# Three more output tiles turned on VectorE from quartered loads, instead of on TensorE: a planner's two thresholds

## The chip, the cores and the metric

The kernel runs on one core of one Trainium2 chip. The metric is the device time of one execution in microseconds (us), given as the median of several runs; lower is better. One further execution was taken with the hardware profiler on, and every row of a profile shown here is of that one.

The engines are named as the profile names them: PE is TensorE (matrix products), PEld its weight loads, DVE is VectorE, ACT is ScalarE, POOL is GpSimd, SP is SyncE. A name with a q at its end (SPq, ACTq) is the engine's queue of instructions that issue transfers (DMAs).

## The reference

One attention layer over a graph of 2708 nodes with 1024 features, all in float32:

```python
def reference(x, adj, W_q, b_q, W_k, b_k, W_v, b_v):
    h = jnp.maximum(_layernorm(x, axis=-1), 0.0)
    q = h @ W_q.T + b_q
    k = h @ W_k.T + b_k
    v = h @ W_v.T + b_v
    z = (1.0 / math.sqrt(1024)) * (q @ k.T)
    z = z * adj                                   # adj: 0 or 1, about 4 ones in a row
    z = jnp.where(z == 0.0, -10000.0, z)
    return x + relu(softmax(z, axis=1) @ v)
```

## The kernel before

**The shape of the work.** A row of `adj` holds about four ones, so no full 2708x2708 product is made. The kernel first finds the ones of each row, sorts the rows by their count, and cuts the sorted rows into 21 tiles of 128 rows (and a short last one). W_q and W_k are multiplied into one matrix M beforehand. From then on each tile t goes through three stages: its query `q = h M` (a product on TensorE), its attention, and its output `relu(u W_v)` plus x (a product on TensorE again).

**Attention of a tile** is VectorE's work. GpSimd gathers the neighbours' rows of h, one neighbour for each of the 128 rows at a time (line 610, a tile `g` of 128x1024, or a free piece of `M`). VectorE forms one score for each gathered tile (line 863), ScalarE the exponentials (line 872), VectorE the weights (lines 906 to 911), ScalarE the first term of the weighted sum (line 912), and VectorE the other terms (line 923). The result is `u`, 128 rows of 1024. A gathered tile lies in one of eleven slots (later thirteen); a slot comes free for the next gather when its term of the sum has been added.

**Products run in units of two tiles.** Twenty units stand in a list: units 0 to 9 make q of two tiles each, units 10 to 19 the output of two tiles each, in the order of the list `order`; the last tile, 8, is done alone behind them. The sixth output pair is unit 15 (tiles 18 and 12), the seventh is unit 16 (tiles 19 and 11). A unit is one level of Strassen's scheme: seven block products of four matmuls of 128x512 (`add_block`, line 1011) instead of eight. Its operands `a11`, `a12`, `a22` and `s1` to `s4` are 128x512 blocks of the two tiles transposed, and their sums (`blocks`). They are made one unit ahead: for unit n+1 the function `upper` runs at step 0 of unit n and `lower` at step 2. The first product that uses them is at step 5 of unit n.

**Two ways to transpose.** `is_faced` decides for each tile:

- By TensorE: eight transposes of 128x128 against the identity (`half_turned`, line 415) into PSUM, and ScalarE copies out (`held`, line 718) for `a11`, `a12` and `a22`; VectorE reads the fourth half from PSUM in its sums (line 722).
- By VectorE ("faced"): VectorE transposes only within 32x32 blocks, so the blocks have to be moved to their places by the transfers. ScalarE permutes the columns of `u` into `v` (line 945), its queue stores `v` to `u_dram` (line 947), SP's queue loads it back by quarters in four transfers of 32x4x256 (`by_quarters`, line 700), and VectorE makes two transposes of 128x512 (`faces`, line 705).

A tile turned by TensorE is handed over in one of two ways. If its unit is at most two units ahead when it is finished (`near`), `u` stays on chip. Otherwise SP's queue stores it (line 951) and loads it back in whole rows (line 1212).

**What sets the order.** VectorE's order is written out by the program: attention is a generator (`attention`), and at each of the seven steps of a unit `advance(share)` takes from it as many steps as the budget `share` allows. The budget is 20.9/7 or 21.5/7 us for a step, less 2.3/7 us for each faced tile of the next unit, whose transposes VectorE has to make in the same stretch:

```python
share = (20.9 if n < len(units) - 5 else 21.5) / 7
if nxt is not None and nxt[0] == "o":
    share -= 2.3 / 7 * len(set(nxt[1:]) & faced_tiles)
```

The other engines' orders are made by a scheduler when the program is built. `load_rows` brings unit n+2's tiles at step 4 of unit n. Whether a tile is faced is settled in `sums`, when the program order reaches its last term: `now` is the unit and step reached there, `unit` the tile's own unit, `len(q_pairs)` is 10.

**The end.** Tile 8 is faced: VectorE's last term for it is at line 929, then ScalarE's copy, the store, four loads, and one transpose into `T_alone` (line 705). TensorE uses `T_alone` first at the `between` of unit 19. Late in unit 19 TensorE also runs a small product `ps_f` (line 1353) from `many`, a count that VectorE makes at lines 1339 to 1351; its result decides whether a general fallback must run.

Of the kernel before, what the change touches and what calls it, by code (L numbers as in the profile page):

```python
# [65 lines left out]
def tile_preln_masked_attention(  # L66
# [144 lines left out]
    def row_tile(name):  # L211
        return work.tile([P, D], FT, tag="row", name=name, bufs=ROWS)
# [626 lines left out]
    def fill():  # L839
        while wanted and free:  # L840
            t, s = wanted.pop(0)
            g = free.pop(0)
            if s == K[t]:
                half = slice(HOSTS.index(t) * HP, (HOSTS.index(t) + 1) * HP)
                nc.gpsimd.dma_start(g[:HP], v_dram[half, :])
            else:
                with tc.issue_after(first_q[0].ins) if first_q else nullcontext():
                    gathered.append(gather(g, h_dram[:, :], t, s, P, skip=True))
            g_of[t].append(g)

    def chained(step):

        with tc.issue_after(chain[-1].ins):
            chain.append(step())
# [64 lines left out]
    def sums(t):  # L919
        u, coef, m = us.pop(t)  # L920
        for s in range(0 if t in EMPTY else 1, K[t]):
            fill()
            chained(lambda: nc.vector.scalar_tensor_tensor(  # L923
                u, g_of[t][s], coef[:, s:s + 1], u, op0=ALU.mult, op1=ALU.add))
            free.append(g_of[t][s])
            yield 1.3
        fill()
        if t in HOSTS:
            chained(lambda: nc.vector.scalar_tensor_tensor(
                u[:HP], g_of[t][K[t]][:HP], m[:HP, 3:4], u[:HP], op0=ALU.mult, op1=ALU.add))  # L930
            free.append(g_of[t][K[t]])
            yield 1.3
            fill()
        g_of.pop(t)
        if t == SECOND:
            nc.sync.dma_start(v_dram, u)
            whole_second.append(True)
            return
        unit = next((n for n, pair in enumerate(units) if pair[0] == "o" and t in pair[1:]), len(units))
        if now < [unit - 2, 2] and unit <= len(q_pairs) + 4 or unit >= len(units) - 1:  # L940
            faced_tiles.add(t)
        print("done", t, "at", now, "unit", unit, t in faced_tiles)
        if t in faced_tiles:
            v = row_tile(f"v_{t}")
            nc.scalar.copy(v.rearrange("p (a c r) -> p c a r", a=QUADS, r=QP),
                           u.rearrange("p (c a r) -> p c a r", a=QUADS, r=QP))
            nc.scalar.dma_start(u_dram[t * P:(t + 1) * P, :], v)
        elif near(t):
            held[t] = u
        else:  # L950
            nc.sync.dma_start(u_dram[t * P:(t + 1) * P, :], u)
        done.add(t)
# [7 lines left out]
    def attention(order):  # L960
        for t in order[:2]:
            ask(t)
        free.extend(slots)

        fetch(order[0])
        fill()
        yield 0.0
        marked(0, EARLY)
        yield 0.0
        after = order[1:] + [None, None]  # L970
        yield from scores(order[0], after[0])
        for i, t in enumerate(order):
            nxt = after[i]
            ahead = nxt is not None and K[t] + K[nxt] <= HIGH + 1
            part = scores(nxt, after[i + 1]) if nxt is not None else iter(())
            if ahead:

                for _ in range(min(2, K[nxt] - 1)):
                    yield next(part, 0.0)
            weights(t)  # L980
            yield 0.6
            if ahead:
                yield from part
            yield from sums(t)
            yield from part
# [8 lines left out]
    spent, now = [0.0], [0, 0]  # L994

    def near(t):

        return t == alone or any(t in unit[1:] for unit in units[:now[0] + 3] if unit[0] == "o")
# [193 lines left out]
    q_pairs = [(t, t + 1) for t in range(0, BARE, 2)]  # L1192
    o_pairs = [(order[i], order[i + 1]) for i in range(0, FULL - 1, 2)]
    alone = order[-1]
    units = [("q",) + p for p in q_pairs] + [("o",) + p for p in o_pairs]
# [367 lines left out]
```

## Time and profile before

| | us |
|---|---|
| median of 3 runs | 638.43 (636.95 to 638.96) |
| the profiled execution, its own time | 638.0 |
| the profiled execution, span from the first to the last instruction | 636.3 |
| TensorE busy | 624.6 (98% of the span) |
| VectorE busy | 525.7 (83%) |
| GpSimd busy | 361.8 (57%) |
| ScalarE busy | 283.5 (45%) |

The granted clock of TensorE is 0.995 over the span. In the timeline an instruction's row begins with its start and its duration in us; "x8" is the number of neighbours merged into the row, and brackets at the end tell how long the engine was idle before it and what ended that. A matmul of 128x512 in float32 shows as two records. A row's duration reaches to the end of its last instruction, so rows of one engine overlap a little: what an instruction holds its engine for is read from one row's start to the next.

### The profile page before, as it was taken

Reading aid. Unit: us, or ns where it says so; the run is one execution under the profiler, and the core shown is the slowest. Engines: PE = TensorE matmul, PEld = TensorE weight load, DVE = VectorE, ACT = ScalarE, POOL = GpSimd, SP = SyncE. Lnnn points to the kernel's source line nnn. Section 1 sums busy time; section 2 is a strip of 40 time slices with the busy share of each in tenths; the row PEclk is TensorE's granted clock in tenths of the full one; section 3 lists DMA queues with packets and bytes.
Section 4 is the critical chain, followed back from the end, with each engine's and each line's share of the span. In section 5 each row is a group of like instructions: output and inputs, shape, how many; then the busy total and the mean of one; then the engine's idle time right before and its main releaser. Section 6 shows DMA issues by size and latency. Waiting matters only on the chain.

```text
span 636.3 us, 6139 instructions
## 1 busy us (share of the span) xinstructions
PE 624.6 (98%) x1627; PEld 315.5 (50%) x1627; DVE 525.7 (83%) x1021; ACT 283.5 (45%) x421; POOL 361.8 (57%) x383
## 2 busy tenths in 40 slices
PE   9999999999999999999999999999999999999994
PEld 5777766444444544444444434444444444444441
DVE  5999889897995755997889999999999989898341
ACT  3539975859667533424341243443343333422300
POOL 2649960975868277563742563576566777632431
PEclk9999999999999999999999999999999999999997
DMA  8998897598696439986699998999999999893761
GB/s 339 407 372 310 334 351 298 199 342 328 246 382 221 170 113 334 326 299 196 194 289 323 297 412 216 311 318 324 351 378 321 334 299 295 242 289 95 210 217 40
DMA packets 62352, 180.11 MB, mean 283 GB/s; under 512 B 10039, under 2 KB 17031, under 8 KB 61672
## 3 DMA queue, kind: packets, MB, share of 16 engines
q0 software_dynamic: 25136, 78.41, 39.4%
q1 hardware_dynamic: 31242, 80.19, 35.8%
q10 hardware_dynamic: 5934, 21.06, 8.5%
q8 instruction: 15, 0.25, 0.2%
q14 instruction: 25, 0.20, 0.1%
HBM read 147.23 MB, written 42.31 MB: 298 GB/s over the span
## 4 chain that ended last, share of the span: by engine, by line
PE 85%; DVE 6%; issue 4%; DMA 3%; SPq 1%; POOL 0%; ACT 0%; POOLq 0%; DVEq 0%; ACTq 0%
PE ps L1011 38%; PE psy L1011 28%; PE ps_y L476 6%; PE ps_x L476 4%; PE ps_z L476 4%; PE pt L415 3%; DVE u L923 2%; DMA g<-h_dram,tab 1%; DMA or<-u_dram 1%; DVE junk L863 1%; DVE s L722 1%; DVE wlow L1270 1%; PE ps_y L511 1%; SPq L700 1%; DVE q L1092 0%
## 5 line engine op out<-in xcount | busy, mean ns | idle before, releaser
L610 POOL DMA_INDIRECT g<-h_dram,tab x94 | 121.4, 1291 | 84.4 <-DVE u L923 31.1
L1011 PE MATMUL ps<-M,a 128*128 128x512 f32 x320 | 144.0, 593 | 0.0
L1011 PE MATMUL psy<-wlow,s 128*128 128x512 f32 x320 | 143.9, 592 | 0.0
L863 DVE SCALAR_TENSOR_TENSOR junk<-g,pq 128x1024 uint8<-128x1024 f32 x93 | 113.7, 1222 | 14.0 <-DMA g<-h_dram,tab 10.9
L1011 PEld LDWEIGHTS ps<-M,a 128*128 128x128 f32 x320 | 59.8, 190 | 70.8 <-issue 70.6
L1011 PEld LDWEIGHTS psy<-wlow,s 128*128 128x128 f32 x320 | 59.7, 190 | 70.2 <-issue 69.4
L923 DVE SCALAR_TENSOR_TENSOR u<-g,coef,u 128x1024 f32<-128x1024 f32 x69 | 88.4, 1281 | 6.9 <-ACT u L912 5.8
L389 DVE FIND_INDEX8 at<-ones,adj 128x8 uint32<-128x685 f32 (+1 forms) x88 | 74.5, 865 | 0.0
L1011 PE MATMUL psy<-wlow,a 128*128 128x512 f32 x160 | 72.0, 593 | 1.4 <-DVE q L1092 1.4
L1011 PE MATMUL ps<-M,s 128*128 128x512 f32 x160 | 72.1, 592 | 0.0
L1011 PE MATMUL ps<-wlow,s 128*128 128x512 f32 x160 | 72.0, 593 | 0.1
L368 ACT ACTIVATE sized<-adj 128x2708 uint8<-128x2708 f32 (+1 forms) x22 | 54.3, 2468 | 7.5 <-DMA adj<-in_adj_dram 6.2
L298 POOL TENSOR_TENSOR hsum<-hsum,x 128x256 f32<-128x256 f32 (+1 forms) x56 | 38.7, 729 | 25.6 <-DVE wlow L444 21.2
L1110 POOL DMA_INDIRECT y<-in_x_dram,tab x19 | 34.8, 1832 | 29.1 <-ACT y L1127 15.9
L1011 PEld LDWEIGHTS psy<-wlow,a 128*128 128x128 f32 x160 | 30.3, 190 | 40.0 <-issue 37.1
L1011 PEld LDWEIGHTS ps<-wlow,s 128*128 128x128 f32 x160 | 30.3, 190 | 38.6 <-issue 37.9
L1011 PEld LDWEIGHTS ps<-M,s 128*128 128x128 f32 x160 | 30.3, 190 | 38.1 <-issue 37.4
L912 ACT ACTIVATE u<-g,coef 128x1024 f32<-128x1024 f32 x18 | 20.7, 1147 | 32.1 <-DVE coef L911 32.1
L808 POOL DMA_INDIRECT out_dram<-y,tab x21 | 25.0, 1188 | 16.4 <-DVE flag L1354 6.1
L626 POOL DMA_INDIRECT tab_dram<-tab,pos_i x22 | 21.9, 995 | 20.7 <-DVE pos_i L689 15.3
L276 ACT ACTIVATE x<-x,r 128x1024 f32<-128x1024 f32 (+1 forms) x22 | 25.9, 1235 | 7.3 <-POOL r L266 7.3
L760 ACT COPY ps<-bp_sb 128x512 f32<-128x512 f32 x42 | 24.5, 595 | 7.2 <-DVE y L1145 6.7
(251 smaller groups left out, 843.5 us busy)
## 6 DMA issues: line engine op xcount, KB each, us to landing
adj<-in_adj_dram SPq DMA_DIRECT2D x21, 1354.0 KB, 11.3
x<-in_x_dram SPq DMA_DIRECT2D x21, 512.0 KB, 3.9
h_dram<-x ACTq DMA_DIRECT2D x21, 512.0 KB, 8.7
u_dram<-v ACTq DMA_DIRECT2D x13, 512.0 KB, 6.4
or<-u_dram SPq DMA_DIRECT2D x52, 128.0 KB, 7.0
q_late<-q SPq DMA_DIRECT2D x12, 512.0 KB, 6.0
pq<-q_late SPq DMA_DIRECT2D x12, 512.0 KB, 8.6
M<-in_wv_dram SPq DMA_DIRECT2D x4, 1024.0 KB
```

The lines of the kernel that those rows point to most:

```text
L276: nc.scalar.activation(xs[i][:n], xs[i][:n], AF.Relu, bias=r[:n, 4, i:i + 1], scale=r[:n, 3, i:i + 1])
L298: small.append(nc.gpsimd.tensor_add(hsum[:n, cols], hsum[:n, cols], xt[:n, cols]))
L368: nc.scalar.activation(sized[:n], a[:n, :, :PW], AF.Abs, accum_out=total[:n, t:t + 1])
L389: nc.vector.max_index(at[:n, k - first_k, g, :], ones[:n, 0:8], a[:n, g, :])
L476: mm = nc.tensor.matmul(bank, a_tile(o + H * a[0], a[1], i), b(o), start=first and o == 0, stop=(o == H - 1), skip_group_check=True)
L610: return nc.gpsimd.indirect_dma_start(out=dst, out_offset=None, in_=src, in_offset=off, bounds_check=N - 1, oob_is_err=False)
L760: nc.scalar.copy(return_[h], row[:, h * NB:(h + 1) * NB])
L808: to = nc.gpsimd.indirect_dma_start(out=out, out_offset=bass.IndirectOffsetOnAxis(ap=ptab.bitcast(U32)[:n, t, SLOTS:SLOTS + 1], axis=0), i ...
L863: chained(lambda: nc.vector.scalar_tensor_tensor(junk, g_of[t][s], 1.0, tq[t], op0=ALU.mult, op1=ALU.mult, accum_out=zall[:, t, s:s + 1]))
L923: chained(lambda: nc.vector.scalar_tensor_tensor(u, g_of[t][s], coef[:, s:s + 1], u, op0=ALU.mult, op1=ALU.add))
L1011: mm = nc.tensor.matmul(bank, a[:, c, :], b[:, c, :], start=False, stop=(c == 3), skip_group_check=True)
L1110: return nc.gpsimd.indirect_dma_start(out=y[:n], out_offset=None, in_=x, in_offset=off, compute_op=ALU.add)
```

## The change

Two numbers in the rule of `sums` are changed:

```diff
         unit = next((n for n, pair in enumerate(units) if pair[0] == "o" and t in pair[1:]), len(units))
-        if now < [unit - 2, 2] and unit <= len(q_pairs) + 4 or unit >= len(units) - 1:
+        if now < [unit - 2, 1] and unit <= len(q_pairs) + 6 or unit >= len(units) - 1:
             faced_tiles.add(t)
```

Before, units 10 to 14 could be faced; now 10 to 16. With the step changed from 2 to 1 the rule takes tiles 18 and 12 (unit 15; finished at unit 12, steps 2 and 6) and tile 19 (unit 16; finished at unit 13, step 3). Tile 11, finished at unit 14, step 1, is not taken and stays with TensorE. Units 10 to 14 and 17 to 19 keep their way of turning.

Since unit 14 now has two faced tiles ahead and unit 15 one, the budget of attention is smaller in those two units, and attention steps move to later places of VectorE's order. Tile 15 is now finished at unit 15, step 0, instead of unit 14, step 5; by then its unit 17 is near, so it is handed over on chip and is not stored and loaded any more.

On TensorE, around units 14 and 15. The rows are matmuls by their outputs and inputs; `or` is a tile loaded back, `u` a tile handed over on chip, `pt` the PSUM tile that takes the transposes. Before:

```order
L1011 MATMUL psy<-wlow,a_2740 128x512 x4
L415 MATMUL pt<-ident,or_2928 128x128 x8
L1011 MATMUL psy<-wlow,s_2879 128x512 x4
L415 MATMUL pt<-ident,or_2930 128x128 x8
L1011 MATMUL ps_2908<-M,a_2856 128x512 x4
L1011 MATMUL ps_2910<-M,s_2881 128x512 x4
L1011 MATMUL psy<-wlow,s_2874 128x512 x4
L1011 MATMUL ps_3058<-M,a_2996 128x512 x4
L1011 MATMUL ps_3060<-wlow,s_3039 128x512 x4
L1011 MATMUL psy<-wlow,a_2872 128x512 x4
L415 MATMUL pt<-ident,or_3089 128x128 x8
L1011 MATMUL psy<-wlow,s_3043 128x512 x4
```

The same place of the changed kernel:

```order
L1011 MATMUL psy<-wlow,a_2742 128x512 x4
L1011 MATMUL psy<-wlow,s_2883 128x512 x4
L1011 MATMUL ps_2914<-M,a_2860 128x512 x4
L1011 MATMUL ps_2916<-M,s_2885 128x512 x4
L1011 MATMUL psy<-wlow,s_2878 128x512 x4
L1011 MATMUL ps_3047<-M,a_3003 128x512 x4
L1011 MATMUL ps_3049<-wlow,s_3024 128x512 x4
L1011 MATMUL psy<-wlow,a_2876 128x512 x4
L1011 MATMUL psy<-wlow,s_3027 128x512 x4
L415 MATMUL pt<-ident,u_2929 128x128 x8
```

Three groups of eight transposes are gone (tiles 18, 12 and 19); tile 11's, the last row, stays. Nothing else moves on TensorE.

On VectorE, in unit 14, where the operands of unit 15 are made. `u` is a running sum of attention, `junk` a score, `a` and `s` operands. Before:

```order
L923 TENSOR_SCALAR u_2923<-M,coef,u_2923 128x1024 x2
L863 TENSOR_SCALAR junk_3008,zall<-g_1413,pq_2963 128x1024
L863 TENSOR_SCALAR junk_3010,zall<-g_1403,pq_2963 128x1024
L906 TENSOR_SCALAR w_2977,m_3018<-w_2977,keys 128x4
L910 RECIPROCAL m_3018<-m_3018 128x1
L911 TENSOR_SCALAR coef<-w_2977,m_3018 128x4
L863 TENSOR_SCALAR junk_3025,zall<-g_1404,pq_2963 128x1024
L722 TENSOR_TENSOR s_3039<-a_3032,pt 128x512
L722 TENSOR_TENSOR s_3041<-a_2996,pt 128x512
L722 TENSOR_TENSOR s_3043<-s_3039,a_2996 128x512
L722 TENSOR_TENSOR s_3045<-a_3003,s_3043 128x512
```

Now:

```order
L923 TENSOR_SCALAR u_2929<-M,coef,u_2929 128x1024
L705 STREAM_TRANSPOSE a_3003<-or_2934 128x4x4x32
L705 STREAM_TRANSPOSE a_3005<-or_2934 128x4x4x32
L923 TENSOR_SCALAR u_2929<-M,coef,u_2929 128x1024
L863 TENSOR_SCALAR junk_3010,zall<-g_1413,pq_2975 128x1024
L863 TENSOR_SCALAR junk_3018,zall<-g_1403,pq_2975 128x1024
L705 STREAM_TRANSPOSE a_3020<-or_2939 128x4x4x32
L705 STREAM_TRANSPOSE s_3022<-or_2939 128x4x4x32
L722 TENSOR_TENSOR s_3024<-a_3020,s_3022 128x512
L742 TENSOR_TENSOR s_3022<-a_3003,s_3022 128x512
L722 TENSOR_TENSOR s_3027<-s_3024,a_3003 128x512
L722 TENSOR_TENSOR s_3029<-a_3005,s_3027 128x512
```

Four transposes have come in; the four sums are as many as before but read no PSUM tile, and the weights and a score (lines 906 to 911, 863) have moved behind them. In unit 15 two transposes come in likewise.

On VectorE at the end, in unit 19: `T_alone`, the results of unit 19 (`y`, `u`, `p`) and the count (`zs`, `many`). Before:

```order
L705 STREAM_TRANSPOSE T_alone<-or_3698 128x4x8x32
L1145 TENSOR_SCALAR y_3703<-ps_3655,y_3703 128x512
L1339 TENSOR_SCALAR zs<-zall,keys 128x352
L1340 TENSOR_TENSOR zs<-zall 128x352
L1341 TENSOR_SCALAR zs<-zs 128x352
L1342 TENSOR_REDUCE many<-zs 128x1
L1155 TENSOR_TENSOR u_3716<-ps_3657,u_3716 128x512
L1349 TENSOR_TENSOR many<-many,deg 128x1
L1145 TENSOR_SCALAR y_3703<-u_3716,y_3703 128x512
L1351 TENSOR_TENSOR many<-many,deg 128x1
L1151 TENSOR_TENSOR p_3691<-psy,p_3691 128x512
L1145 TENSOR_SCALAR y_3704<-p_3691,y_3704 128x512
```

Now:

```order
L705 STREAM_TRANSPOSE T_alone<-or_3681 128x4x8x32
L1145 TENSOR_SCALAR y_3686<-ps_3638,y_3686 128x512
L1155 TENSOR_TENSOR u_3699<-ps_3640,u_3699 128x512
L1339 TENSOR_SCALAR zs<-zall,keys 128x352
L1145 TENSOR_SCALAR y_3686<-u_3699,y_3686 128x512
L1151 TENSOR_TENSOR p_3674<-psy,p_3674 128x512
L1340 TENSOR_TENSOR zs<-zall 128x352
L1145 TENSOR_SCALAR y_3687<-p_3674,y_3687 128x512
L1341 TENSOR_SCALAR zs<-zs 128x352
L1342 TENSOR_REDUCE many<-zs 128x1
L1349 TENSOR_TENSOR many<-many,deg 128x1
L1351 TENSOR_TENSOR many<-many,deg 128x1
```

The last step of `many` (line 1351) now stands behind the sum into `y_3687`, the second tile of unit 19, and with it behind the gather of x for that tile; before it stood ahead of it.

## The prediction

> **What bounds the kernel now.** I read the page's busy times and chain first, then TensorE's waits and its timeline, then busy times by unit, then VectorE's waits, and last the end of the program. From the page:
>
> ```profile
> span 636.3 us, 6139 instructions
> ...
> PE 624.6 (98%) x1627; PEld 315.5 (50%) x1627; DVE 525.7 (83%) x1021; ACT 283.5 (45%) x421; POOL 361.8 (57%) x383
> ...
> PE 85%; DVE 6%; issue 4%; DMA 3%; SPq 1%; POOL 0%; ACT 0%; POOLq 0%; DVEq 0%; ACTq 0%
> ```
>
> TensorE is the bound: 98% busy, and 85% of the chain that ended last. After 360 us it waits once (its waits from 360 us to the end: us in total, times, longest):
>
> ```profile
> PE psy L1011 <- DVE q L1092: 1.4, 1, 1.4
> ```
>
> That wait is for a q, so it lies before unit 10, where the program's order is the same in both kernels, and it stays. Unit 14's first steps in TensorE's timeline, with the transposes of tiles 18 and 12 in between:
>
> ```profile
> 468.78 1.04 PE L415 MATMUL pt<-ident,or 128*128 128x128 f32 x8
> 469.65 3.60 PE L1011 MATMUL psy<-wlow,s 128*128 128x512 f32 x8
> 473.09 1.04 PE L415 MATMUL pt<-ident,or 128*128 128x128 f32 x8
> 473.96 3.60 PE L1011 MATMUL ps<-M,a 128*128 128x512 f32 x8
> ```
>
> Whatever TensorE no longer does here shortens the program, if TensorE still waits for nothing. VectorE is the engine to watch. Busy times of unit 13, of unit 14, of units 14 to 17 together and of unit 18 (after the stretch and its length come PE, PEld, DVE, ACT, POOL, then PE's granted clock, the DMA engines' share, GB/s):
>
> ```profile
> 444.70:468.80 24.10, 24.10 (x58) 10.61 (x57) 23.01 (x41) 7.99 (x14) 14.01 (x10) 1.00 1.04 370
> 468.80:494.60 25.80, 25.80 (x74) 12.31 (x73) 23.55 (x40) 9.73 (x17) 18.05 (x15) 1.00 1.01 328
> 468.80:571.90 103.10, 103.10 (x289) 49.21 (x288) 93.86 (x145) 38.26 (x65) 67.90 (x53) 1.00 0.96 302
> 571.90:595.90 24.00, 24.00 (x57) 10.64 (x56) 19.76 (x36) 8.26 (x13) 5.96 (x4) 1.00 0.45 114
> ```
>
> Units 14 to 17 turn two tiles each on TensorE and take 103.1/4 = 25.8 us each; units 13 and 18 turn none and take 24.0 to 24.1. TensorE is busy in all of it. VectorE is busy 93.9 of the 103.1 us (91%): it has little room. The DMA engines' share is 0.96 to 1.04 up to unit 17, so transfers are tight too.
>
> **TensorE: what goes.** Three groups of eight transposes. A group holds TensorE from 468.78 to 469.65, and from 473.09 to 473.96: 0.87 us each. Three groups are **2.6 us**. The units agree: 25.8 less 24.0 to 24.1 is 1.7 to 1.8 for two groups. By the records' own mean the answer is another:
>
> ```profile
> L415 PE MATMUL pt<-ident,or 128*128 128x128 f32 x32 | 4.1, 272 | 0.0
> ```
>
> 24 x 272 ns would be 6.5 us. But the records overlap: eight of them pass in 0.87 us, 109 ns each. I take the starts, since they add up to the unit's length, and keep 6.5 for a rival. [...]
>
> **VectorE: what comes.** Two transposes of 128x512 for each tile. Tiles 17 and 13, unit 14's, take this way already and show the price:
>
> ```profile
> 447.23 1.30 DVE L705 STREAM_TRANSPOSE a<-or 128x512 f32<-128x512 f32 x2
> 448.45 1.18 DVE L863 SCALAR_TENSOR_TENSOR junk<-g,pq 128x1024 uint8<-128x1024 f32 x1
> ...
> 452.68 0.71 DVE L705 STREAM_TRANSPOSE a<-or 128x512 f32<-128x512 f32 x1 [0.49 <-DMA or<-u_dram]
> ```
>
> From 447.23 to 448.45 is 1.22 us for a tile, 3.66 us for three (1.22/8 = 153 ns for each 128x128). The sums of `lower` are as many as before. So VectorE has 3.66 us more, in front of everything it still does for attention. Will tile 8, the last, be late by that? Only as far as VectorE's waits don't shrink. The waits of VectorE between 470 and 592 us, grouped (us in total, times, longest):
>
> ```profile
> DVE u L923 <- ACT u L912: 2.8, 2, 1.6
> DVE junk L863 <- DMA M<-h_dram,tab: 1.8, 1, 1.8
> DVE junk L863 <- DMA g<-h_dram,tab: 1.8, 2, 1.0
> DVE p L1122 <- ACT taken L1076: 1.2, 2, 1.0
> DVE s L722 <- ACT a L718: 1.0, 1, 1.0
> ```
>
> The last two groups hang on TensorE's pace, through ScalarE's copies of its results: 1.2 + 1.0 = 2.2 us. A VectorE that is later, beside a TensorE that is earlier, no longer has them. The two for gathers are 1.8 + 1.8 = 3.6 us. A later VectorE finds them landed, but it also frees the slots later; I take half, 1.8. The first group is two round trips to ScalarE and stays. So 2.2 + 1.8 = 4.0 us can be given back, a little more than the 3.66 that come, and tile 8 ends about when it ends now. Call its lateness d: bounds -2.1 (all of 5.8 given back) and +3.7 (nothing given back); I take 0, near the -0.3 that these rows give.
>
> **The end: what d costs.** Here TensorE comes 2.6 us earlier to something that VectorE and a chain of transfers deliver:
>
> ```profile
> 591.14 1.27 DVE L929 SCALAR_TENSOR_TENSOR u<-g,m,u 64x1024 f32<-64x1024 f32 x1
> ...
> 605.03 1.25 DVE L705 STREAM_TRANSPOSE T_alone<-or 128x1024 f32<-128x1024 f32 x1 [11.56 <-DMA or<-u_dram]
> ...
> 607.75 0.53 DVE L1341 SCALAR_TENSOR_TENSOR zs<-zs 128x352 f32<-128x352 f32 x1
> ...
> 609.26 0.19 PEld L1011 LDWEIGHTS ps<-M,T_alone 128*128 128x128 f32 x1 [0.24 <-issue]
> ...
> 610.07 0.15 DVE L1351 TENSOR_TENSOR many<-many,deg 128x1 f32<-128x1 f32 x1
> 610.14 0.68 DVE L1151 TENSOR_TENSOR p<-psy,p 128x512 f32<-128x512 f32 x1
> 610.86 0.69 DVE L1145 SCALAR_TENSOR_TENSOR y<-p,y 128x512 f32<-128x512 f32 x1
> ...
> 616.55 0.28 PE L1353 MATMUL ps_f<-many,ones 128*128 128x1 f32 x2
> ```
>
> `T_alone` is ready at 605.03 + 1.25 = 606.3; TensorE loads it at 609.3, a margin of 3.0. With TensorE 2.6 earlier (606.7) the margin is **0.4 us**. TensorE then stalls for d - 0.4 us, and the gain is 2.6 less that. At d = 0 it is whole.
>
> **Small terms, each costed at nothing.** `many` moves behind `y<-p`, which needs x's gather. That row ran at 610.86 without a wait, so the gather had landed; behind it come 0.7 for the sum itself, about 0.5 each for lines 1341 and 1342 and 0.15 each for lines 1349 and 1351, 2.0 in all, so `many` ends at about 612.9, and TensorE comes to `ps_f` at 616.55 - 2.6 = 613.9. Cover 1.0 us; with a late d it is gone too, but the stall at `T_alone` has then pushed TensorE back by as much. ScalarE loses five copies and gains three, and is busy 38.3 of the 103.1 us. SP's queue issues twelve quarter loads instead of four stores and four row loads, without the stores' waits for VectorE in front of its `pq` loads. The quarters have from step 4 of unit 13 (about 458.5, 4/7 into the first row of units above) to unit 14 (468.8): 10 us; tiles 17 and 13 have the same path now and cost the 0.49 of the row above. If a load took the longest seen, d would grow by some 5:
>
> ```profile
> DMA to landing us min/median/max: 3.1/7.0/15.1
> ```
>
> Traffic is near even: three tiles go as 1 KB pieces instead of rows, and tile 15's store and load are gone. GpSimd has the same gathers and adds, some in another order.
>
> **The sum.** The profiled execution took 638.0 (span 636.3, 1.7 around it), 0.4 below the median of 638.43. Its time becomes 638.0 - 2.6 = 635.4; against the median, 638.43 - 2.62 = **635.8 us**. About 0.3% (1.9 us) is what a measurement of this kernel can tell from no change. The gain is 0.41%, so a stall of 0.7 us (d = 1.1) already turns "faster" into "the same".
>
> **Rivals.**
> - *VectorE gives back less* (chance 0.29, the same within 0.3%). If gather waits stay because slots come free later, d = 3.66 - 2.2 = 1.5, the stall 1.1, the time 636.9. If nothing is given back, d = 3.7, the stall 3.3, the time 639.1. For it: VectorE would be busy 97.5 of the 100.5 us that units 14 to 17 then take. Against the worse of the two: the waits on TensorE's pace must shrink when TensorE comes earlier.
> - *The gathers fall behind* (0.16, slower). Units 14 and 15 have less attention in their budget, slots come free later, GpSimd's gathers start later on DMA engines that are full, and VectorE waits for them again after its transposes. The longest wait for a gather is in this row:
>
> ```profile
> DVE junk L863 <- DMA g<-h_dram,tab: 10.9, 5, 5.1
> ```
>
> One such wait in units 15 to 17 makes d = 1.5 + 5.1 = 6.6, the stall at `T_alone` 6.2, the time 638.43 - 2.62 + 6.2 = 642.0. It decides from d = 4.9 on (stall 4.5, 1.9 over the gain). Against it: the longest wait for a gather in these units now is 1.8. A TensorE stall of this length might also lower the granted clock; the wait of 1.4 us did not (1.00 in every row behind it).
> - *A transpose holds TensorE for its record's 272 ns* (0.03): 6.5 us go, and if `T_alone` kept up the time would be 631.9. Against it: the starts. [...]
> - That the change does nothing is excluded by the order: 24 transposes are gone.
>
> **How the numbers follow.** Forecast 0.52 (stall up to 0.7: 635.8 to 636.5), giving with the third rival 0.55 for faster; 0.29 the same; 0.16 slower. The range goes from 634.8 (the forecast less 1.0, the scatter of the runs around their median) to 639.4 (the first rival's 639.1 and a little of the second); about 0.06 lies below and 0.13 above.
>
> **What would show it.** Right: units 14 and 15 take 24.1 and 24.9 us in the windows; three rows of `pt` fewer; VectorE's waits for `a L718` and `taken` between 470 and 592 are gone; line 929 ends within 1 us of 592.4; TensorE has no idle time before `ps<-M,T_alone`. Wrong: line 929 ends over 1.1 us later and TensorE's row of `T_alone` shows a wait for DVE (first rival); a wait of several us on `g<-h_dram` between 490 and 570 (second); TensorE waiting at `ps_f` (my cover for `many`); a wait on `or<-u_dram` at about 470 (the quarters).

## The result and the profile after

| | before | after |
|---|---|---|
| median of 8 runs each, us | 638.34 (636.95 to 640.85) | 641.87 (638.33 to 643.78) |
| profiled execution, us (span) | 638.0 (636.3) | 638.33 (636.6) |
| TensorE busy, us | 624.6 | 623.0 |

The ratio is 1.0052, 95% interval 1.0039 to 1.0065: slower by half a per cent. The profiled execution of after happens to be the shortest of its eight; it shows why even that one gains nothing. Of the longer executions of this kernel none was profiled; two experiments (e3 and e6) caught one of theirs, and the rest is read there.

TensorE's busy times by unit in after, for units 13, 14, 15, 14 to 17 together and 18 (columns as in the prediction):

```profile
444.70:468.80 24.10, 24.10 (x58) 10.71 (x57) 22.27 (x40) 9.33 (x15) 12.96 (x10) 1.00 1.05 335
468.80:492.80 24.00, 24.00 (x58) 10.61 (x57) 20.30 (x32) 6.94 (x12) 16.68 (x12) 1.00 1.04 303
492.80:517.70 24.90, 24.90 (x66) 11.41 (x65) 23.97 (x41) 8.25 (x14) 17.72 (x15) 1.00 0.93 282
468.80:569.30 100.50, 100.50 (x266) 46.68 (x265) 93.27 (x144) 35.02 (x60) 69.85 (x53) 1.00 0.98 293
569.30:593.30 24.00, 24.00 (x58) 10.61 (x57) 22.12 (x34) 6.31 (x11) 5.75 (x3) 1.00 0.45 124
```

Units 14 to 17 take 100.5 us instead of 103.1: the 2.6 us are saved as forecast. In the last two columns stands something that was not forecast: in unit 13 the DMA engines are as busy as before (1.05, before 1.04) but move 335 GB/s instead of 370.

The waits of after, TensorE's from 360 us on, then VectorE's between 470 and 592 us:

```profile
PE ps L1011 <- DVE T_alone L705: 1.4, 1, 1.4
PE psy L1011 <- DVE q L1092: 0.8, 1, 0.8
PE ps_f L1353 <- DVE many L1351: 0.8, 1, 0.8
```

```profile
DVE a L705 <- DMA or<-u_dram: 3.2, 2, 2.2
DVE u L923 <- ACT u L912: 2.8, 2, 1.6
DVE junk L863 <- DMA g<-h_dram,tab: 0.5, 1, 0.5
```

TensorE has two new waits, at `T_alone` and at `ps_f`. VectorE has lost its waits on TensorE's pace and nearly all for gathers, and has a new one for the quarter loads of unit 15's tiles. The end of the program on TensorE, before and then after:

```profile
606.25 3.60 PE L1011 MATMUL psy<-wlow,s 128*128 128x512 f32 x8
609.69 3.60 PE L1011 MATMUL ps<-M,T_alone 128*128 128x512 f32 x8
...
616.55 0.28 PE L1353 MATMUL ps_f<-many,ones 128*128 128x1 f32 x2
```

```profile
603.55 3.60 PE L1011 MATMUL psy<-wlow,s 128*128 128x512 f32 x8
608.56 3.70 PE L1011 MATMUL ps<-M,T_alone 128*128 128x512 f32 x8 [1.42 <-DVE T_alone L705]
612.10 3.60 PE L1011 MATMUL psy<-wlow,a 128*128 128x512 f32 x8
616.45 0.35 PE L1353 MATMUL ps_f<-many,ones 128*128 128x1 f32 x2 [0.75 <-DVE many L1351]
```

By starts TensorE is 2.70 us early at the last product before `T_alone`, 1.13 early at `T_alone` and 0.10 early at `ps_f`: the whole saving is gone within 13 us, even in the shortest of the eight.

### The profile page after: what moved, and what is told of

It is laid out like the page before. It is cut to its first block, busy times and chain, and to the rows that moved or that the text cites. A ratio compares the mean times of both kernels' runs of the same rounds, so it can differ in the third digit from the quotient of the medians.

```text
span 636.6 us, 6107 instructions
## 1 busy us (share of the span) xinstructions
PE 623.0 (98%) x1603; PEld 313.1 (49%) x1603; DVE 529.1 (83%) x1027; ACT 283.6 (45%) x419; POOL 363.4 (57%) x383
## 4 chain that ended last, share of the span: by engine, by line
PE 46%; DMA 21%; issue 15%; DVE 11%; POOL 5%; ACT 1%; SPq 0%; POOLq 0%; DVEq 0%; ACTq 0%
PE ps L1011 17%; PE psy L1011 11%; DMA g<-h_dram,tab 7%; PE ps_y L476 6%; DMA or<-u_dram 5%; PE ps_x L476 4%; PE ps_z L476 4%; DMA out_dram<-y,tab 4%; DVE junk L863 4%; DVE u L923 3%; POOL g L610 2%; PE pt L415 2%; DMA M<-h_dram,tab 2%; DVE s L722 1%; DMA v_dram<-u 1%
## 5 line engine op out<-in xcount | busy, mean ns | idle before, releaser
L1110 POOL DMA_INDIRECT y<-in_x_dram,tab x19 | 33.5, 1765 | 31.1 <-ACT y L1127 23.3
L808 POOL DMA_INDIRECT out_dram<-y,tab x21 | 26.9, 1281 | 12.4 <-DMA y<-in_x_dram,tab 5.8
L945 ACT COPY v<-u 128x1024 f32<-128x1024 f32 x16 | 16.7, 1045 | 35.4 <-DVE u L923 31.1
```

The source lines that it names most:

```text
L808: to = nc.gpsimd.indirect_dma_start(out=out, out_offset=bass.IndirectOffsetOnAxis(ap=ptab.bitcast(U32)[:n, t, SLOTS:SLOTS + 1], axis=0), i ...
L1110: return nc.gpsimd.indirect_dma_start(out=y[:n], out_offset=None, in_=x, in_offset=off, compute_op=ALU.add)
```

## Experiments

Ratios are to the kernel before on the same chip. The runs fell on chips whose before-medians were 637.8 to 637.9 (the first eight runs) and 639.5 to 639.8 (the others), so ratios are compared, not times.

| run | what differs | ratio (95%) |
|---|---|---|
| e1 | the change, once more | 1.0061 (1.0038 to 1.0084) |
| e2 | change; tile 8 by TensorE | 1.0023 (1.0001 to 1.0044) |
| e3 | change; `many` earlier | 1.0093 (1.0075 to 1.0112) |
| e4 | change; both of these | 1.0028 (1.0007 to 1.0049) |
| e6 | unit 15's two tiles alone | 1.0056 (1.0034 to 1.0077) |
| e7 | unit 16's tile 19 alone | 1.0000 (0.9991 to 1.0009) |
| e8 | change; tail store on ScalarE's queue | 1.0041 (1.0022 to 1.0059) |
| e9 | change; unit 15's loads earlier | 1.0137 (1.0114 to 1.0159) |
| e10 | change; unit 15 loaded whole | 0.9993 (0.9972 to 1.0013) |
| e11 | change; unit 15 loaded by 4 x 32 rows | 1.0043 (1.0020 to 1.0066) |
| e12 | before; unit 15's row loads cut | 1.0075 (1.0050 to 1.0100) |
| e13 | change; unit 15's transposes later | 1.0074 (1.0045 to 1.0102) |
| e14 | change; unit 15's stores cut, loads whole | 1.0052 (1.0035 to 1.0069) |
| e15 | e14; tile 8 by TensorE | 1.0042 (1.0026 to 1.0058) |
| e16 | as e14, tile 19 too | 1.0114 (1.0086 to 1.0142) |
| e18 | e16; tile 8 by TensorE | 1.0100 (1.0077 to 1.0124) |
| e20 | e10 and six loads of 16 bytes | 0.9995 (0.9976 to 1.0013) |
| e21 | change; unit 15 loaded by 2 x 64 rows | 1.0039 (1.0018 to 1.0060) |

### The end of the program: e1 to e4

e1 is the changed kernel, unedited. e2 hands tile 8 to TensorE:

```diff
-        if now < [unit - 2, 1] and unit <= len(q_pairs) + 6 or unit >= len(units) - 1:
+        if now < [unit - 2, 1] and unit <= len(q_pairs) + 6 or unit == len(units) - 1:
...
-            if nxt is None and i == 1:
-                ...
-                faces(uT, single["rows"], 0, DC)
+            if nxt is None and i == 4:
+                single["turned"] = turned(single["rows"], "alone")
```

e3 moves the block that makes `many` from behind the last unit to right behind tile 8's last term; e4 does both.

> The changed kernel once more, for a second profile beside that of its fastest run (638.3) and for more times; before is 638.3. Theory A (VectorE ends tile 8 late, and TensorE waits for T_alone): 641 to 643, and a profile that is slower than the first shows a longer wait for T_alone, 4 to 6 us instead of 1.4. Theory B (the count many, which now stands behind the gather of x for the last tile of unit 19, holds TensorE at ps_f): the wait at ps_f grows from 0.8 to 4 to 5 us and the one for T_alone stays near 1.4. Theory C (units 14 to 17 themselves are slower at times): waits of TensorE between 470 and 593 us, or a lower clock there.

> The changed kernel with tile 8 turned by TensorE from the chip: no copy, store, quarter loads and VectorE transpose of T_alone, but eight transposes more on TensorE (0.9 us) ahead of the last product of unit 19. Theory A: the wait for T_alone goes and with it nearly all of the loss: 638.3 - 2.6 + 0.9 + at most 0.8 at ps_f = 636.6 to 637.4. Theory B: ps_f still waits, 641 to 642. Theory C: 641 to 643.

> The changed kernel with the whole count (lines 1339 to 1351) put behind VectorE's last term for tile 8, into the time in which VectorE waits for T_alone's loads, so that ps_f no longer waits for the gather of x. Theory A: T_alone still comes late: 640.5 to 643, no better than the changed kernel by more than 1. Theory B: 638.3 - 2.6 + 1.4 = 637 to 638. Theory C: 641 to 643.

> The changed kernel with both edits: tile 8 turned by TensorE, and the count early. Theories A and B: 638.3 - 2.6 + 0.9 = 636.6, the same as with one of the edits alone (the one that the true theory names). If both waits hide each other, only this one is fast: 636.6 here against 640 and more with either edit alone. Theory C: 641 to 643.

With tile 8 on TensorE, though one group of transposes comes back, the ratio falls from 1.0061 to 1.0023 (the intervals overlap by a little), and e4 beside e3 says the same clear of noise (1.0028, 1.0093): the `T_alone` chain is where part of the loss reaches the end. Both stay above the 636.6 to 637.4 us that theory A gave, so it is not all of it. Making `many` earlier brings nothing in e4, and e3 is no better than the change: the wait at `ps_f` is not the cause. What e3 brought is its profile, one of a longer execution (642.43 us, span 640.7). Its order is that of the change on ScalarE, GpSimd and the queues, and on VectorE up to tile 8's last term. VectorE's waits at unit 15's transposes there, and then TensorE's waits from 360 us on:

```profile
476.32 1.30 DVE L705 STREAM_TRANSPOSE a<-or 128x512 f32<-128x512 f32 x2 [6.45 <-DMA pq<-q_late]
...
483.83 0.71 DVE L705 STREAM_TRANSPOSE a<-or 128x512 f32<-128x512 f32 x1 [2.58 <-DMA or<-u_dram]
```

```profile
PE psy L1011 <- ACT taken L1076: 3.0, 1, 3.0
PE ps L1011 <- DVE T_alone L705: 1.5, 1, 1.5
PE ps L1011 <- DVE s L722: 0.6, 1, 0.6
```

The first transpose reads only `or`, tile 18's quarters; the row names the `pq` load because that uses a semaphore of theirs next. In e1's profile the same row starts at 472.43, after a wait of 2.84. The starts of VectorE's line 911 in the two traces agree within 0.3 us up to 461, then e3's are 4.06 to 4.07 later in every row to the end: one event separates these two executions, and it is this wait. Theory C, that units 14 to 17 themselves are slower at times, has it right for e3. VectorE stands in order, so the result sums behind it come late, ScalarE's copy `taken` behind those, and TensorE stands for it:

```profile
492.79 5.30 PE L1011 MATMUL psy<-wlow,a 128*128 128x512 f32 x8 [3.04 <-ACT taken L1076]
497.93 3.60 PE L1011 MATMUL psy<-wlow,s 128*128 128x512 f32 x8
```

### Which tile, and where in SP's queue: e6 to e9

From here on theory A is that the quarter loads of unit 15 land late, and theory B that VectorE's added work alone is too much. e6 and e7 set the thresholds for a part of the tiles; e8 and e9 keep all and move what stands ahead of unit 15's loads:

```diff
# e6
-... and unit <= len(q_pairs) + 6 or unit >= len(units) - 1:
+... and unit <= len(q_pairs) + 5 or unit >= len(units) - 1:
# e7
+... and unit <= len(q_pairs) + 6 and unit != len(q_pairs) + 5 or unit >= len(units) - 1:
# e8
-                nc.sync.dma_start(tail_dram, ya[P - 1:, :])
+                nc.scalar.dma_start(tail_dram, ya[P - 1:, :])
# e9
-                if i == (2 if n in (FIRST, last_q) else 4) and n + 2 > FIRST ...
+                if i == (2 if n in (FIRST, last_q) else 3 if n == 13 else 4) and n + 2 > FIRST ...
```

> Thresholds changed so that only unit 15's tiles (18 and 12) go to VectorE; tile 19 stays with TensorE. TensorE saves 2 x 0.87 = 1.74 us. Theory A (the quarter loads of unit 15 land late, VectorE's queue stands behind them): the wait for the loads at 470 to 477 us stays at 1 to 6 us, the runs scatter over 4 us as those of the full change, median 640 to 643. Theory B (VectorE's added work alone is too much): 2.44 us more instead of 3.66, so tile 8 is at most 2.4 later, the stall at T_alone at most 2.4 - (3.0 - 1.74) = 1.1, the time 636.2 to 637.4 with the small scatter of the kernel before.

> Only tile 19 of unit 16 goes to VectorE; unit 15 stays with TensorE. TensorE saves 0.87 us. Theory A: its four loads have a unit of time and nothing of unit 15's eight in front of them, so there is no wait above 1 us, the scatter is that of the kernel before, and the time is 637.0 (637.9 less 0.87), up to 637.9. Theory B gives about the same here (1.22 us more for VectorE, margin at T_alone 2.1): 637.0. A time above 639 would mean that tile 19's part alone does the harm, against both.

> The changed kernel, with one store (tail_dram, line 1130, one row of 4 KB) issued from ScalarE's queue instead of SP's. SP's queue then has no wait for y in front of the eight quarter loads of unit 15. Theory A: they are issued before 459 instead of from 461, land by 470, VectorE's wait at 471 falls below 1 us, the slow group of runs (642 to 643) is gone, and the time is 635.5 to 637.5. Theory B: the wait goes, but VectorE's work stays, tile 8 stays over 2 us late and the time stays at 638 to 642.

> The changed kernel, with unit 15's loads written at step 3 of unit 13 instead of step 4: on SP's queue the eight quarter loads then stand ahead of the tail_dram store instead of behind it; some gathers and scatters of GpSimd change places too. Theory A: as with the store on ScalarE's queue, loads landed by 468, no slow group of runs, 635.5 to 637.5. Theory B: 638 to 642. If this one is fast and the one with the store on ScalarE's queue is not (or the other way), the harm lies in where GpSimd's transfers stand, not in the wait of SP's queue.

Unit 15's two tiles alone cost as much as the whole change; tile 19 alone costs nothing and gains nothing measurable. e6's profile is again of a longer execution, with the same rows (6.89 us at the first transpose, 3.0 at `taken`). The DMA columns split the two in unit 13; e6 and then e7:

```profile
444.70:468.80 24.10, 24.10 (x57) 10.64 (x56) 22.32 (x40) 8.18 (x15) 13.07 (x10) 1.00 1.05 333
```

```profile
444.70:468.80 24.10, 24.10 (x57) 10.45 (x55) 22.82 (x41) 9.03 (x15) 13.81 (x10) 1.00 1.04 370
```

e8 did less than expected (1.0041): the wait at 471 was gone, as theory A has it, but its trace has these instead between 465 and 592 us:

```profile
DVE junk L863 <- DMA g<-h_dram,tab: 2.6, 2, 2.2
DVE a L705 <- issue: 1.6, 1, 1.6
```

On full DMA engines (share 1.04 in unit 13) loads that go earlier seem to push the gathers back (0.5 us of waits for them in after, 2.6 here). TensorE stands 2.45 us at `T_alone` in this trace, and its granted clock is 0.79 from 608 to 616 us (last section). e9 went against theory A altogether. Its loads had landed (no wait at the first transpose), but ScalarE came to stand 9 us for an output scatter, and TensorE for ScalarE:

```profile
494.37 0.60 ACT L1119 ACTIVATE y<-ps 128x512 f32<-128x512 f32 x1 [8.99 <-DMA out_dram<-y,tab]
```

In e9 some of GpSimd's gathers and scatters change places too, so it does not price the loads alone.

### The loads alone, VectorE's work alone: e10 to e13

e10 and e11 keep the change and cut unit 15's loads otherwise; e12 is the kernel before with its two row loads cut; e13 places the transposes a step later:

```diff
# e10
+                if t in faced_tiles and t in units[15][1:]:
+                    faced.append(rows[-1])
+                    nc.sync.dma_start(rows[-1], u_dram[t * P:(t + 1) * P, :])
# e11, in place of the last line
+                    for a in range(QUADS):
+                        nc.sync.dma_start(rows[-1][a * QP:(a + 1) * QP, :],
+                                          u_dram[t * P + a * QP:t * P + (a + 1) * QP, :])
# e12, in the kernel before
+                elif t in units[15][1:]:
+                    for a in range(QUADS):
+                        cols = slice(a * D // QUADS, (a + 1) * D // QUADS)
+                        nc.sync.dma_start(rows[-1][:, cols], u_dram[t * P:(t + 1) * P, cols])
# e13, and likewise 3 instead of 2 for the second tile
+                if i == (3 if n == 0 else 4 if turn else 1 if n == 14 else 0):
```

> The changed kernel, but unit 15's two tiles are loaded in whole rows by one transfer of 512 KB each (pieces of 4 KB) instead of four quarters of 32x4x256 (pieces of 1 KB). VectorE transposes them as before; the blocks are then not where they belong, so that these two tiles' output is not the reference's. Everything but the loads stays: TensorE's 24 transposes are gone, VectorE has its six. Theory A (the harm is the quarter loads' late landing): VectorE's first wait at 471 falls from 1 to 7 us to below 1, the slow group of runs (642 to 643) is gone, the time is 635.5 to 637.5. Theory B (VectorE's added 3.66 us are the harm): 640 to 642.5 as the full change.

> As the run with whole rows, but each of the two tiles by four transfers of 32 rows (128 KB each, pieces of 4 KB): as many transfers as in the full change, in the same places of every queue; only the pieces are larger. These two tiles' output is not the reference's. If the size of the pieces is what delays the loads (1 KB pieces moved 15 bytes per ns of a DMA engine in the trace of the change between 445 and 493 us, 4 KB pieces of the same queue 24): 635.5 to 637.5, no slow group. If the number of transfers is (each holds one of the eight semaphores that SP's queue goes round, so its later issues wait): 640 to 642.5 as the full change. Theory B: 640 to 642.5.

> The kernel before, with unit 15's two row loads each cut into four transfers of 128 rows by 256 columns (pieces of 1 KB); all else as before: TensorE turns the tiles, VectorE has no new work. Theory A: the loads land late here too, TensorE now stands at its transposes at 468.8 us for 1 to 6 us, and the time is 639 to 643 with the wide scatter of the full change. Theory B: 637.9, no change.

> The changed kernel with unit 15's transposes placed one step later on VectorE (the first tile's at step 1 of unit 14 instead of 0, the second's at step 3 instead of 2), so that a term and a score of attention stand ahead of the first wait and the weights and two scores ahead of the second. Theory A: 3.4 us more for the loads to land before VectorE stands; the waits at the loads fall by 2 to 3.5 us, the time to 637 to 640. Theory B: no change, 640 to 642.5. If the loads' delay comes from DMA engines that are full, part of it returns as waits for gathers, as in the run with the store on ScalarE's queue.

e12 settles one half: with no new work on VectorE and none taken from TensorE, cutting these loads makes the kernel before slower by 0.75%, and TensorE now stands at its own transposes:

```profile
PE pt L415 <- DMA or<-u_dram: 4.8, 4, 1.8
```

e10 settles the other: with VectorE's transposes in and the loads whole, the time is that of before. Theory B is out as the cause of the slowdown, though not of the missing gain (below). e10's executions still scatter (637.0 to 644.2), and its profile is of a longer one (643.65). Unit 15's transposes wait for nothing in it. It is 3.2 us late before it comes to anything that the change touches (line 911 at 401.28 instead of 398.10), and at the end TensorE stands 3.06 us at `T_alone`, and the product behind that shows 5.40 us in its row, where before's shows 3.60:

```profile
613.46 5.40 PE L1011 MATMUL ps<-M,T_alone 128*128 128x512 f32 x8 [3.06 <-DVE T_alone L705]
```

e11, whose order on every engine is that of the change, shows that small pieces are not needed for the harm. e13 was a miss: the transposes stand later, but the waits for loads did not shrink (3.44 and 2.53 us in its profile), and it is no faster than the change; TensorE waits 2.2 us for the later operands `s` and 2.6 us at `T_alone`, and beyond that I have no explanation.

### Cut stores instead of cut loads: e14 to e18

```diff
+            if t in units[15][1:]:                       # e16, e18: + units[16][1:]
+                cut = u_dram[t * P:(t + 1) * P, :].rearrange("(a r) (g j) -> g r a j", r=QP, g=QUADS)
+                for g in range(QUADS):
+                    nc.scalar.dma_start(cut[g], v[g * QP:(g + 1) * QP, :].rearrange("r (a j) -> r a j", a=QUADS))
```

The loads of these tiles are whole rows; e15 and e18 have e2's edit too.

> The changed kernel, with the cut into 32x4x256 quarters moved from the loads of unit 15's two tiles to their stores: ScalarE's queue stores each in four transfers of 32x4x256, and SP's queue loads whole rows, one transfer a tile. The result is the reference's. Bytes, pieces of 1 KB and the number of transfers are the same as in the full change, but the cut ones run 10 us earlier, where nobody waits, and only two large loads are left in front of VectorE's transposes. Theory A1 (what harms is how long the loads take that VectorE waits for, and how many stand in SP's queue): as the run with whole rows, ratio 0.995 to 1.000. Theory A2 (the bytes in small pieces load the DMA engines, wherever they run): waits for gathers take the place of those for the loads, ratio 1.003 to 1.006.

> The same, and tile 8, the last, turned by TensorE from the chip: no T_alone chain of copy, store, loads and VectorE transpose any more, one group of transposes (0.87 us) back on TensorE. By the trace the T_alone wait was 1.4 to 2.5 us. If VectorE's lateness reaches the end only through that chain, this takes 0.5 to 1.6 us off the run without it: ratio 0.994 to 0.998.

> As the run with cut stores for unit 15, and tile 19 of unit 16 likewise: its four loads (which in the trace of the change stood until 14 to 16 us after their issue) become one. Theory A1: equal or 0.1% better than with unit 15 alone, since VectorE did not wait for tile 19's loads in most traces. Theory A2: no difference.

> Cut stores for units 15 and 16, and tile 8 turned by TensorE: the candidate for a version that beats both. Theory A1: ratio 0.993 to 0.997 (of 2.6 us saved, 0.87 given back, 0.4 of the rest lost). Theory A2: 1.000 to 1.003, as the run with tile 8 on TensorE alone had.

The ratio is theory A2's, but not by A2's way: the waits that came are not for gathers. Unit 15's transposes no longer wait; unit 14's do, 25 us earlier:

```profile
453.93 1.30 DVE L705 STREAM_TRANSPOSE a<-or 128x512 f32<-128x512 f32 x2 [4.75 <-DMA or<-u_dram]
...
462.16 0.71 DVE L705 STREAM_TRANSPOSE a<-or 128x512 f32<-128x512 f32 x1 [3.27 <-issue]
...
479.10 1.30 DVE L705 STREAM_TRANSPOSE a<-or 128x512 f32<-128x512 f32 x2
```

These runs do not price the cut stores alone. In all four the edit also moved a third `pq` load in front of unit 14's quarter loads on SP's in-order queue, and the quarter loads are issued some 11 us later. e14, then after:

```profile
417.70 21.49 SPq L833 DMA_DIRECT2D pq<-q_late  x3
439.28 12.95 SPq L700 DMA_DIRECT2D or<-u_dram  x8
```

```profile
427.94 11.59 SPq L700 DMA_DIRECT2D or<-u_dram  x8
```

Whether the `pq` load or the cut stores beside them make unit 14's loads late stays open. e16 missed both theories: with tile 19's store cut too the ratio is 1.0114, and TensorE stands 4.6 us at `taken`. With the stall that early, e15 and e18 gain only 0.1% by tile 8 on TensorE, which is not clear of noise.

### Number of transfers or the cut itself: e20 and e21

In the changed program SP's and ScalarE's transfers take eight semaphores in turn, and an issue waits for the last transfer that used its own. SP's order, with the semaphores that an issue waits for (`DMAHW7` was last taken by the store of tile 19):

```
L700 DMA or_2934<-u_dram 32x4x256 [waits DMAHW4_49]
L700 DMA or_2939<-u_dram 32x4x256 [waits DMAHW5_49]
L700 DMA or_2939<-u_dram 32x4x256 [waits DMAHW6_49]
L700 DMA or_2939<-u_dram 32x4x256 [waits DMAHW7_49]
```

After's trace has SP's queue wait 2.3 us at line 700 for `u_dram<-v`, a store that these loads do not read. e20 keeps that (as many transfers, the same waits), but without bytes; e21 halves the tile:

```diff
# e20, behind the whole-row load of e10, each issued after the one before
+                    for a in range(1, QUADS):
+                        load = nc.sync.dma_start(tiny[0:1, k:k + 4], u_dram[t * P:t * P + 1, 0:4])
# e21, in place of the whole-row load
+                    for a in range(0, P, P // 2):
+                        nc.sync.dma_start(rows[-1][a:a + P // 2, :], u_dram[t * P + a:t * P + a + P // 2, :])
```

> As the run with whole rows (one transfer of 512 KB for each tile of unit 15, output of these two tiles not the reference's), with three loads of 16 bytes behind each: as many transfers on SP's queue as in the full change, and the same waits for the eight semaphores, but no bytes in them. Theory N (the number of transfers: later ones wait for the one eight before to land): slower than before, ratio 1.003 to 1.006, as with four transfers of 32 rows. Theory L (what counts is how long the transfers take that carry a tile, when four issues share it): 0.997 to 1.001, as the run with whole rows.

> As the run with whole rows, but two transfers of 64 rows for each tile (four in all; output of these two tiles not the reference's): between one transfer a tile (ratio 0.9993) and four (1.0043). Theory N: about half way, 1.000 to 1.003. Theory L: nearer to one transfer, 0.997 to 1.001. A ratio of 1.004 or more would speak against both, for something in the whole-row run other than the number of its transfers.

The number is not it: e20 is as fast as before. e21 came out at 1.0039, above what either theory gave it: two halves harm about as much as four parts (1.0043). So it is the cut of the load itself, not in proportion to the number of its parts. e10, e20 and e21 share the same one small difference in GpSimd's order, so that is not it either. The traces, one of each, show where the time goes. From line 911 near 398 us to line 929's last start VectorE takes 193.0 us before, 196.4 in e10 and 196.3 in e20, but 199.0 in e11 and 198.9 in e21 (the change itself 195.7 and 196.3 in the short executions of after and e1, 200.4 in e3). In e11 and e21 the smaller part of this is waiting for the cut loads; the larger is for gathers. VectorE's waits in e11 between 465 and 592 us (e21 has 5.8 and 1.1; e20 follows below):

```profile
DVE junk L863 <- DMA g<-h_dram,tab: 5.8, 4, 3.1
DVE a L705 <- DMA or<-u_dram: 1.2, 1, 1.2
```

e20's unit 13, and its waits of VectorE between 465 and 592 us and of TensorE from 360 us on:

```profile
444.70:468.80 24.10, 24.10 (x57) 10.45 (x55) 22.76 (x40) 8.57 (x14) 13.62 (x10) 1.00 1.04 365
```

```profile
DVE junk L863 <- DMA g<-h_dram,tab: 3.2, 1, 3.2
DVE u L923 <- ACT u L912: 2.8, 2, 1.6
```

```profile
PE ps L1011 <- DVE T_alone L705: 2.2, 1, 2.2
```

No wait for unit 15's loads, 365 GB/s against 335; yet the profiled time is 638.02, that of before: a gather wait has come in and TensorE stands 2.2 us at `T_alone`. So loads that cost nothing bring the kernel back to the time before, and no further. (In e10, e11, e20 and e21 the blocks of unit 15's tiles do not come where they belong, so none of them is a version to use.) e10 with tile 8 on TensorE, which would show whether the stall at `T_alone` is all of the missing gain, was not run.

No version tried beats the kernel before.

## Why the prediction was wrong

**The step that failed: "Small terms, each costed at nothing", the quarter loads.** The prediction gave them 10 us, from step 4 of unit 13 (458.5) to 468.8, and expected the 0.49 us wait of the unit before. They were issued only from 461.55 on, since they stand on SP's in-order queue behind the `tail_dram` store, which waits for ScalarE:

```profile
SPq L1130 <- ACT y L1127: 8.7, 1, 8.7
...
SPq L700 <- DMA u_dram<-v: 2.3, 1, 2.3
```

I had credited this queue with losing its waits for VectorE and not looked at the store that stays in front. Nor was the comparison with tiles 17 and 13 a fair one. The profile before shows both: their quarter loads, and unit 15's row loads, which stand behind the same store:

```profile
430.49 7.86 SPq L700 DMA_DIRECT2D or<-u_dram  x8
460.85 0.80 SPq L1212 DMA_DIRECT2D or<-u_dram  x2
```

The quarters of tiles 17 and 13 had 16.7 us from their first issue to their first transpose (447.23), those of unit 15 have 8.85 us in after until VectorE is ready for them (470.40). Whole rows need no more than that: issued at 460.85 before and at 461.30 and 462.65 in e20, they kept nobody waiting. So it is the cut loads that the time left was too short for. In the shortest execution the loads then cost 3.2 us of waits, in e3's and e6's profiles 9.0 and 8.9. "If a load took the longest seen, d would grow by some 5" had the right size: line 929's last start is 2.55 late in after's profile, 3.2 in e1's, 7.27 in e3's and 7.45 in e6's. It was kept out of the sum and given no chance of its own. 14 of the 21 executions of after, e1 and e6 took over 641 us; that the unprofiled ones among them are long in the same way is likely, but not shown.

**What the late loads cost.** The prediction let lateness act only at `T_alone`. In the longer executions of e3 and e6 it acts 120 us earlier; in e3: 3.04 us at `taken`, plus a product that takes 5.14 us from start to start (492.79 to 497.93) instead of 3.43, at a granted clock of 0.79 (492 to 500 us). By starts TensorE in e3 is 5.15 us behind e1 there (497.93 against 492.78), and 4.25 at `T_alone` (613.86 against 609.61), where e3 waits 0.9 less.

**"I take 0, near the -0.3 that these rows give": also wrong.** The waits were given back as assumed and better (2.2 on TensorE's pace, 3.1 of 3.6 for gathers), but other waits took their place: in after the quarter loads (3.2), in e20 a gather (3.2). d was 2.55 in after, 3.4 in e20 and 3.2 in e1; only e7, with one transposed tile, has 0.02. That is the first rival's place, "VectorE gives back less", with its stall of 1.1 to 3.3 (measured at `T_alone`: 1.4 in after, 2.4 in e1, 2.2 in e20, 3.1 in e10), and its verdict, the same as before, holds for the short executions and for e10 and e20.

**The cover of 1.0 us for `many`** was 0.75 short in the shortest execution: `y<-p` ahead of it had to wait 2.49 us, so the row that had run "without a wait" no longer did. It cost time in that one; by e3 and e4 it is not what slows the median.

**The second rival** gave 642.0 for gathers that fall behind, and the median is 641.87, but by another way: in after the gather waits between 470 and 592 us are 0.5 instead of 3.6. Waits for gathers come where those for unit 15's loads shrink: 2.6 us in e8, 3.2 in e20, 5.8 in e11 and e21. In these last two the way is the rival's own.

**Right:** the 2.6 us on TensorE, priced by starts and not by the records' mean, and 1.22 us for a tile on VectorE (the row at 471.38 to the next at 472.61: 1.23). "Traffic is near even" was right in bytes and wrong as a cost: bytes moved per busy time of the DMA engines fell by a tenth in unit 13.

**Open:** why the DMA engines move less in the same busy time when a tile's load is cut by rows, in four or in two; why a cut by columns harms without that (e12 moved 363 GB/s in its unit 13); and what makes the quarters land at 472 in one execution and 476 in the next.

## What to carry to other kernels

Before a transfer is put on the path of a busy in-order engine, read from the trace what stands ahead of it on its own queue, and how long transfers of that size take in that very stretch; here, at a DMA share of 1.04 to 1.05, cutting loads cost 0.4 to 0.75% at equal bytes. When an engine with little room gets more work, look for the waits that take the place of those that vanish (here, with VectorE 91% busy, 5.3 us went and 3.2 us came): a lateness taken as zero needs a reason, not a balance. When executions of a changed kernel scatter more than those of the old one, look for a trace of each sort and for the first row in which they part.

## What the runs showed of the hardware

**Behind waits of 2.4 to 3.0 us TensorE's granted clock was lower in some traces, and the length alone does not decide.** e3 in the windows before, at and after its wait of 3.04 us:

```profile
468.80:492.00 23.20, 20.87 (x49) 8.72 (x47) 13.79 (x24) 4.48 (x7) 11.67 (x9) 1.00 0.94 287
492.00:500.00 8.00, 7.21 (x13) 3.22 (x14) 7.86 (x11) 2.57 (x6) 6.63 (x5) 0.79 0.71 143
500.00:510.00 10.00, 10.00 (x31) 4.85 (x30) 9.82 (x19) 4.48 (x8) 8.17 (x7) 1.00 0.95 310
```

The granted clock is 0.79 over the 8 us from 492 to 500, and the product behind the wait takes 1.7 us more than 3.43 from start to start. Two waits of equal length at `T_alone` part here, e8's and then e11's; the product behind the first takes 5.09 us from start to start, that behind the second 3.53:

```profile
609.90 5.25 PE L1011 MATMUL ps<-M,T_alone 128*128 128x512 f32 x8 [2.45 <-DVE T_alone L705]
```

```profile
614.92 3.70 PE L1011 MATMUL ps<-M,T_alone 128*128 128x512 f32 x8 [2.45 <-DVE T_alone L705]
```

The granted clock is 0.79 from 608 to 616 us in e8 and 1.00 from 613 to 621 in e11. It is lower behind 2.4 us of waiting at `taken` in e14 too (0.93 from 468.8 to 493 us), and in e9, whose wait of 8.28 us ends at 495.64, it is 0.50 from 492 to 500 us; in e1, with 2.43 us at `T_alone`, it is 1.00 from 600 to 620 us. What decides between equal waits is not shown by these runs.

**Cut loads and the DMA engines.** In the packet records between 444.7 and 493 us, a 4 KB piece of SP's queue took 170 to 177 ns in e10 and e20 (whole rows) and 209 to 211 ns in e11 and e21 (four and two transfers a tile), and the quarters' 1 KB pieces moved 15 bytes per ns in after, against 24 for 4 KB pieces. Over unit 13, its window set in each trace by that trace's own line 911, the engines moved 368 and 364 GB/s in e10 and e20, 339 and 342 in e11 and e21, at a share of 1.04 to 1.05 in all four. Why the pieces take longer is not shown: a load of e11 or e21 reaches 32 or 64 partitions, but e12's loads, which each reach all 128, harm too (1.0075).
